# Attention, then a GRU, on one core: v of fourteen batches by seven quarter products, x normalised in place, and one root moved

## The chip, the cores and the metric

The kernel runs on one core of one Trainium2 chip. The metric is the device time of one execution in microseconds (us). TensorE (PE) multiplies, VectorE (DVE), ScalarE (ACT) and GpSimd (POOL) do the element work, and SyncE (SP) issues the transfers. Everything is float32.

## The reference

The input `x` has 16 batches of 256 tokens with 512 features; `cond` has one row of 512 for each batch. An adaptive normalisation and an attention with 16 heads of 32 come first, then a GRU over the 256 tokens:

```python
scale, shift = split(cond @ W_emb + b_emb)
xn = rms_norm(x, g_norm) * (1 + scale) + shift
q, k, v = split_heads(xn @ W_qkv)              # 512 -> 3 * 512
attn = softmax(rms_norm(q, g_q) @ rms_norm(k, g_k).T * 32 ** -0.5)
o = merge_heads(attn @ v)
x = x + o + o @ W_out

def cell(h, x):                                # scanned over the tokens
    r, z, n = gates(x @ W_ih + b_ih, h @ W_hh + b_hh)
    return (1 - z) * n + z * h
x = x + scan(cell, cond, x)
```

## The kernel before

The program has two parts. The attention part takes the first third of the time and goes batch by batch; the GRU part takes the rest, one token after the other. The order on PE, DVE, ACT and POOL is written out by hand: each engine does its instructions in the order in which the source issues them, and waits where data or a buffer is not ready. Transfers go through SP's queue in their order of issue.

In the attention part, the loop over `b` runs four slots for each batch, one for each group of four heads. A slot begins with the logits of its group (`logits_by_key`, L703), whose exponentials ScalarE takes (`exps_by_key`, L717), while GpSimd adds the two halves of each exponential (`sums`, L719). The group of the slot before (`prev`) is weighed with v (`weigh_by_key`, L731, L741), and VectorE divides by the sum: two transposes and a reciprocal (`put_weighed_by_key`, L755 to L759), and the product into `oT` (`finish_weighed_by_key`, L765). That last step frees the PSUM bank X of the weighing.

Beside this, each slot prepares part of the next batch `m = b + 1` and the turning of batch `b + 2`. From batch 2 on, q and k are not projected directly. The product of 256 tokens by 512 features with the weights is cut into halves in each direction, and seven products of quarters (`multiply`, L346) take the place of eight, after the scheme of Strassen and Winograd. The sums that this takes stand in `w_sums` (of the weights, made once: `make_w_sum`) and `x_sums` (of x, four for each batch, S1 to S4: `make_x_sum`, L336), all by GpSimd. `keep` (L358) copies partial results from PSUM, `add_kept` (L363) adds them. The next batch's first product `z` goes to PSUM bank A, `q7` to bank Y, `q2` to bank X. v is projected directly (`project`, L269): 32 matmuls of 128x512 a batch.

The quarters of q and k are normalised by head. ScalarE squares them (`square`, L390), VectorE sums the squares (`sum_heads`, L394). The root (`Rsqrt`) has a first half (L190 on VectorE, L192 and L193 on ScalarE) and a second half of three small VectorE operations (L197, L198, L200, named `u` and `y`). `norm_quarters` then multiplies (L373), transposes into `qkT` (L379), and lets GpSimd scale (L386).

x itself: `load_x` loads a batch, `norm_first` (L216) squares and sums it on ScalarE, `norm_apply` (L227) writes the normalised x to a buffer `xs` in `w_a`, `turn_x` (L242) transposes it on TensorE, and `put_x` (L259, L261) scales and shifts it into `xnT`. In `w_a` the halves of `squares` are the output of the squares of q and k; the squares of x, of which only the sum is used, go to `xs`.

The gains decide at run time whether the exponentials are bounded; with the inputs used they are, and of the two programs in the file the one with `bounded` true runs.

Of the kernel before, what the change touches and what calls it, by code (L numbers as in the profile page):

```python
# [20 lines left out]
def kernel(  # L21
# [99 lines left out]
    def program(ctx, bounded):  # L121
# [4 lines left out]
        small = work.enter_context(tc.tile_pool(name="small", bufs=4))  # L126
# [12 lines left out]
        xs = w_a[:, KC * 2 * D : KC * 2 * D + NT * D].rearrange("p (n d) -> p n d", n=NT)  # L139
        squares = w_a[:, KC * 2 * D + NT * D : KC * 3 * D].rearrange("p (i n) -> p i n", i=2)  # L140
        wih = w_a.rearrange("p (k n) -> p k n", k=KC)
        w_sums = w_a[:, 0 : 3 * 2 * D].rearrange("p (i k c) -> p i k c", i=3, k=2)
        x_sums = w_a[:, 3 * 2 * D : 4 * 2 * D].rearrange("p (i k t) -> p i k t", i=4, k=2)

# [64 lines left out]
        def norm_first(b, parts=range(NT)):  # L209
            if parts[0] == 0:  # L210
                batches[b].ssx = small.tile([P, NT], F32, tag="ssx", name=f"ssx_{b}")
                batches[b].rs = Rsqrt(batches[b].ssx, D, NT, f"x{b}")
            for n in parts:

                unused = xs[:, n, :] if b != 2 else spare(f"squares_{n}")
                nc.scalar.activation(  # L216
                    unused, x_tiles[b][n], AF.Square,
                    accum_out=batches[b].ssx[:, n : n + 1],
                )
# [5 lines left out]
        def norm_apply(b, rstd):  # L225
            for n in range(NT):
                nc.vector.tensor_scalar(  # L227
                    xs[:, n, :], x_tiles[b][n], rstd[:, n : n + 1],
                    None, ALU.mult,
                )  # L230
            if 0 < b and b + 2 < B:
                load_x(b + 2)
# [11 lines left out]
        def turn_x(b, banks):  # L244
            batches[b].xnT = p1.tile([P, KC, T], F32, tag="xnT", name=f"xnT_{b}", bufs=2)
            tps = [tile_ps(f"tpx_{b}_{r}", banks[r], (P, KC, NT, QR)) for r in range(R)]
            for c in range(KC):
                for n in range(NT):
                    turn_block(
                        [tp[:, c, n, :] for tp in tps], xs[:, n, c * P : (c + 1) * P]  # L250
                    )
            return tps
# [55 lines left out]

        T2, T3, T4, T1 = range(4)
# [6 lines left out]
        def make_w_sum(i):  # L316
            if i == T3:
                add_weights(w_sum(T3), w_half(1, 1), ALU.subtract, w_half(0, 1))
            elif i == T2:
                add_weights(w_sum(T2), w_sum(T3), ALU.add, w_half(0, 0))  # L320
            elif i == T4:
                add_weights(w_sum(T4), w_half(1, 0), ALU.subtract, w_sum(T2))
            else:
                add_weights(w_half(0, 1), w_half(0, 1), ALU.subtract, w_half(0, 0))
# [13 lines left out]
        def multiply(a, stationary, w, name=None):  # L338
            start = isinstance(a, str)
            if start:  # L340
                a = tile_ps(name, a)
            w = w.rearrange("p k s (g j d) -> p k j s g d", j=HG, d=DH)
            for k in range(2):
                for i in range(4):
                    for j in range(HG):
                        nc.tensor.matmul(  # L346
                            a[32 * j : 32 * j + 32, i * P : (i + 1) * P],
                            stationary[:, k, 32 * i : 32 * i + 32],
                            w[:, k, j],
                            start=(start and k == 0 and i == 0),  # L350
                            stop=(k == 1),
                            skip_group_check=True,
                        )
            return a

# [32 lines left out]
        def square(b, n, s, a):  # L388
            sq = spare(f"sq_{b}_{n}_{s}") if b == 0 else squares[:, s]
            nc.scalar.activation(sq, a, AF.Square)  # L390
            return sq
# [357 lines left out]
        def put_weighed_by_key(w, finish=True):  # L749


            if w is None:
                return
            den = p1.tile([P, T // DH, DH], F32, tag="den", name=f"den_{w.b}_{w.g}")
            nc.vector.transpose(den.rearrange("p a b -> p (a b)"), w.o[:, 1, :])  # L755
            inv = small.tile([P, T // DH, 1], F32, tag="inv", name=f"inv_{w.b}_{w.g}")
            nc.vector.reciprocal(inv, den[:, :, 0:1])
            rden = p1.tile([P, T], F32, tag="rden", name=f"rden_{w.b}_{w.g}")
            nc.vector.transpose(rden, inv.to_broadcast([P, T // DH, DH]))  # L759
            w.rden = rden  # L760
            if finish:
                finish_weighed_by_key(w)
# [23 lines left out]
        def first_slot1(b, w, prev, st):  # L786
            m = b + 1
            exps_by_key(w)
            make_w_sum(T2)
            project_qk(m, 0, 1, (3,), st.k)  # L790
# [11 lines left out]
        def first_slot2(b, w, prev, st):  # L802
# [8 lines left out]
            for i in (S3, S1, S2, S4):  # L811
                make_x_sum(m + 1, i)
            put_weighed_by_key(prev)
# [32 lines left out]

        def quarter_slot0(b, w, prev, st):
# [3 lines left out]
            project(b, 1, 2, (2, 3), st.v1)  # L851
            put_v(b, 1, st.v1)
            tpx = turn_x(b + 2, ("lg2", "lg3")) if b + 2 < B else None
            put_weighed_by_key(prev)
            if tpx:
# [11 lines left out]
        def quarter_slot1(b, w, prev, st):  # L867
            m = b + 1
            exps_by_key(w)
            multiply(st.z, x_sums[:, S1], w_half(0, 1))  # L870
            weigh_by_key(prev, "X")
            z4 = keep(m, 4, st.z)
            st.c22 = add_kept(m, 1, 1, st.q7, z4)
            put_weighed_by_key(prev)
            multiply(st.z, x_sums[:, S4], w_half(1, 1))
            sq = st.sa.square(1, st.c22)
            st.v0 = project(m, 0, 2, (0,), "Z")
            if m + 1 < B:
                make_x_sum(m + 1, S3)
            st.sa.add(1, sq)  # L880
# [7 lines left out]
        def quarter_slot2(b, w, prev, st):  # L888
# [11 lines left out]
            project(m, 0, 2, (1, 2, 3), st.v0)  # L900
            if m + 1 < B:
                make_x_sum(m + 1, S1)
                make_x_sum(m + 1, S2)
            st.sb.add(1, sq)
            finish_weighed_by_key(prev)
            if b + 3 < B:
                batches[b + 3].rs.first()
            put_v(m, 0, st.v0)
            st.sb.rs.first()
            st.rb = st.sb.rs.second()  # L910
            if b == 2:
# [4 lines left out]
        def quarter_slot3(b, w, prev, st):  # L916
# [3 lines left out]
            weigh_by_key(prev, "X")  # L920
            st.v1 = project(m, 1, 2, (0, 1), "Z")
# [3 lines left out]
            if m == B - 1:  # L925
# [3 lines left out]
                load_rows(wih, w_ih)  # L929
                project(m, 1, 2, (2, 3), st.v1)  # L930
                put_v(m, 1, st.v1)
            else:
                make_x_sum(m + 1, S4)
                begin_quarters(m + 1, st)
# [143 lines left out]
        def fast_last_batch(prev):  # L1078
            w = logits_by_key(B - 1, 0)
            for g in range(NG):  # L1080
                exps_by_key(w, sums=False)
                weigh_by_key(prev, "YZ"[g % 2], sums=(g == 0))
# [18 lines left out]
        with tc.manual_schedule(engines=ORDERED):  # L1101
# [29 lines left out]
            load_x(2)  # L1131
            tpx = turn_x(0, ("lg0", "lg1"))
            emb = small.tile([P, 8, 32], F32, tag="emb", name="emb", bufs=1)
# [36 lines left out]
            norm_first(2)  # L1170
            if bounded:
                batches[2].rs.first()
            turn_qk(0, 1, norm_qk(0, 1, accs[1], s1.rs.second()))
# [27 lines left out]
            (fast_last_batch if bounded else last_batch)(prev)  # L1201
# [226 lines left out]
```

## Time and profile before

| | before |
|---|---|
| median of 3 runs | 1636.08 us (1634.75 to 1636.09) |
| the profiled execution | 1636.28 us, span 1634.4 us |
| granted TensorE clock | 0.998 |
| logits of the first batch begin | 36.12 us |
| period of a batch, from b = 1 on | 29.91 us (one of 29.99) |
| first product of the GRU part (L944) | 500.9 us |
| busy in the 29.90 us from 251.05 | PE 29.90, DVE 21.32, ACT 17.43, POOL 16.90 us |

A row of the profile's lists names an engine, a line of the program, the operation, output<-inputs and their sizes. A float32 matmul leaves two rows. The lengths of TensorE's rows overlap, so the time that a group costs is read from its start to the start of the next group.

### The profile page before, as it was taken

The page shows a single profiled execution, that of the slowest core. Times are in us where ns is not written, and L with a number is a line of the kernel's source. Part 1 is how long each engine was busy: PE and PEld are TensorE (multiplying, and loading weights), DVE is VectorE, ACT ScalarE, POOL GpSimd, SP SyncE. Part 2 cuts the span into 40 slices and gives each one's busy share as a digit, 9 for nine tenths or more (in the row PEclk, how much of TensorE's full clock was granted, in tenths as well). Part 3 has the DMA queues.
Part 4 walks back from the last instruction along what each step waited for, and adds up shares of the span by engine and source line. Part 5 has one row for each costly group of instructions (what it writes and reads, how often), then busy time and mean ns, then how long its engine had stood idle before and what let it go on. Part 6 is the DMA issues. An engine that isn't in the chain of part 4 may idle for free.

```text
span 1634.4 us, 99580 instructions
## 1 busy us (share of the span) xinstructions
PE 1616.0 (99%) x45590; PEld 1308.3 (80%) x45590; DVE 954.2 (58%) x3102; ACT 560.8 (34%) x1770; POOL 342.5 (21%) x626
## 2 busy tenths in 40 slices
PE   8999999999999999999999999999999999999997
PEld 4566766767767888888888888888888888888886
DVE  4677677676665555555555555555555555555554
ACT  3565665565643222222222222222222222222222
POOL 0655556465550000000000000000000000000000
PEclk9999999999999999999999999999999999999999
DMA  5100001000042000000000000000000000000000
GB/s 217 29 17 22 24 16 29 16 16 27 18 116 70 11 23 21 20 17 17 18 23 23 18 17 17 20 21 23 17 18 17 21 20 17 10 11 11 17 11 18
DMA packets 51409, 44.71 MB, mean 27 GB/s; under 512 B 10615, under 2 KB 43683, under 8 KB 50979
## 3 DMA queue, kind: packets, MB, share of 16 engines
q1 hardware_dynamic: 50889, 38.20, 8.6%
q8 instruction: 358, 5.87, 1.5%
q14 instruction: 72, 0.59, 0.1%
q10 hardware_dynamic: 90, 0.06, 0.0%
HBM read 29.79 MB, written 8.39 MB: 23 GB/s over the span
## 4 chain that ended last, share of the span: by engine, by line
PE 68%; DVE 1%; issue 0%; ACT 0%; DVEq 0%; POOL 0%; ACTq 0%
PE gr L983 27%; PE gz L983 20%; PE gn L983 14%; PE o L1217 6%; PE first L944 0%; PE lg L703 0%; PE o L731 0%; DVE trh L1266 0%; PE o L741 0%; ACT n L1345 0%; DVE n L1344 0%; DVE n L1343 0%; DVE padded L1372 0%; DVE padded L1371 0%; DVE padded L1373 0%
## 5 line engine op out<-in xcount | busy, mean ns | idle before, releaser
L983 PE MATMUL gr<-w_a,xT 128*32 128x256 f32 x4096 | 267.7, 379 | 0.0
L1339 ACT ACTIVATE r<-trr 128x64 f32<-128x64 f32 x256 | 65.4, 256 | 514.4 <-DVE trr L1266 512.6
L1266 DVE STREAM_TRANSPOSE trr<-gr 128x128 f32<-128x128 f32 x256 | 81.0, 317 | 274.7 <-PE gr L983 274.6
L719 POOL TENSOR_TENSOR sums<-e 128x256 f32<-128x256 f32 x240 | 183.0, 793 | 221.8 <-ACT e L717 221.8
L983 PEld LDWEIGHTS gr<-w_a,xT 128*32 128x32 f32 x4096 | 132.8, 110 | 85.1
L1345 ACT ACTIVATE n<-n 128x64 f32<-128x64 f32 x256 | 65.6, 256 | 309.2 <-DVE n L1344 306.3
L1375 POOL TENSOR_TENSOR y<-xT,padded 128x64 f32<-128x64 f32 x128 | 41.1, 321 | 531.5 <-DVE padded L1373 531.5
L1266 DVE STREAM_TRANSPOSE trh<-gn 128x128 f32<-128x128 f32 x256 | 81.0, 317 | 117.3 <-PE gn L983 117.3
L717 ACT ACTIVATE e<-lg 128x512 f32<-128x512 f32 x256 | 131.9, 603 | 45.5 <-PE lg L703 45.3
L1217 PE MATMUL o<-oT,wo 128*32 128x256 f32 x1920 | 147.2, 379 | 0.0
L1375 POOL TENSOR_TENSOR y<-xT,h 128x64 f32<-128x64 f32 x127 | 40.7, 320 | 501.0 <-DVE h L1373 501.0
L983 PE MATMUL gr<-w_b,padded 128*32 128x128 f32 x4096 | 135.7, 273 | 2.4 <-DVE padded L1373 1.4
L983 PEld LDWEIGHTS gr<-w_b,padded 128*32 128x32 f32 x4096 | 114.6, 110 | 29.1 <-DVE padded L1373 28.6
L983 PE MATMUL gz<-w_b,padded 128*32 128x128 f32 x4096 | 135.3, 273 | 0.0
L983 PE MATMUL gn<-w_b,padded 128*32 128x128 f32 x4096 | 135.3, 273 | 0.0
L983 PE MATMUL gz<-w_a,xT 128*32 128x128 f32 x4096 | 135.3, 273 | 0.0
L983 PE MATMUL gr<-w_b,h 128*16 128x128 f32 x4064 | 134.3, 273 | 0.5 <-DVE h L1373 0.2
L983 PEld LDWEIGHTS gz<-w_a,xT 128*32 128x32 f32 x4096 | 117.1, 110 | 21.8
L983 PE MATMUL gz<-w_b,h 128*16 128x128 f32 x4064 | 134.2, 273 | 0.0
L983 PE MATMUL gn<-w_b,h 128*16 128x128 f32 x4064 | 134.2, 273 | 0.0
L269 PE MATMUL qkv<-w_b,xnT 128*32 128x512 f32 x1024 | 122.1, 596 | 0.1
L983 PEld LDWEIGHTS gn<-w_b,padded 128*32 128x32 f32 x4096 | 114.5, 110 | 0.0
(154 smaller groups left out, 2540.2 us busy)
## 6 DMA issues: line engine op xcount, KB each, us to landing
xin<-in_x_dram SPq DMA_DIRECT2D x256, 32.0 KB, 2.7
out_dram<-osb SPq DMA_DIRECT2D x248, 32.0 KB, 2.5
x<-in_x_dram SPq DMA_DIRECT2D x28, 256.0 KB, 2.9
w_b<-in_L_cond_W_qkv_dram SPq DMA_DIRECT2D x4, 768.0 KB, 8.5
w_a<-in_L_cond_W_ih_dram SPq DMA_DIRECT2D x16, 192.0 KB, 6.6
w_a<-in_L_cond_W_emb_dram SPq DMA_DIRECT2D x4, 512.0 KB, 5.3
w_b<-in_L_cond_W_hh_dram SPq DMA_DIRECT2D x16, 128.0 KB, 4.1
oT<-in_x_dram SPq DMA_DIRECT2D x2, 512.0 KB, 8.6
```

Source lines behind the costliest of these rows:

```text
L269: nc.tensor.matmul(a[32 * j : 32 * j + 32, :], batches[b].xnT[:, k, n * P + 32 * j : n * P + 32 * j + 32], wq[:, k, s * D : (s + 1) * D], ...
L717: nc.scalar.activation(w.e[i], w.lg[i], AF.Exp)
L719: nc.gpsimd.tensor_tensor(w.sums[:, i, :], w.e[i][:, 0, :], w.e[i][:, 1, :], ALU.add)
L983: nc.tensor.matmul(dst[32 * j : 32 * j + rows], stationary, w[:, k, :].rearrange("p (g j c) -> p j g c", g=3, c=P)[:, j, first::2][:, : ds ...
L1217: nc.tensor.matmul(acc[32 * j : 32 * j + 32, :], w[:, k, P * j + 32 * m : P * j + 32 * m + 32], rhs, start=(k == 0), stop=(k == KC - 1),)
L1266: nc.vector.transpose(tr.rearrange("p q s b -> p (q s b)"), gate)
L1339: nc.scalar.activation(r, turned("r", t, gr[:, 0, :])[:, :, s, :], AF.Sigmoid)
L1345: nc.scalar.activation(n, n, AF.Tanh)
L1375: (nc.gpsimd if t + 1 < T else nc.vector).tensor_tensor(y[:, :, tl * B : (tl + 1) * B], xTs[grp][:, :, ti, :], h, ALU.add)
```

## The change

v of the batches 2 to 15 is formed by seven quarter products too. `multiply_v` does one: eight matmuls of 128x256. `w_sums_v` holds three sums of v's weights, made once on GpSimd in the first two batches. The seven products are spread over the slots: two each in slots 1, 2 and 3, the last (`end_v`) in slot 0 of the batch itself. `keep_v` copies three partial results from PSUM on ScalarE, GpSimd adds the first of them to two others, and VectorE forms three quarters of v (`add_v` and slot 3). The next batch's `z` in slot 3 stands between the fifth and the sixth v product. In slot 1 the last step of the weighing is issued after the sum of squares instead of before.

The room for `w_sums_v` comes from `xs`: x is normalised in place, and the squares of x go into the buffers of the squares of q and k, one in `w_a` and one in a pool. Batch `b + 2`'s buffer is loaded anew after `turn_x` instead of after `norm_apply`. In the first part, the first half of the third x's root stands behind the norm of the second half of the tokens. `emb` and `rden` share the buffer of `den`.

```diff
-        xs = w_a[:, KC * 2 * D : KC * 2 * D + NT * D].rearrange("p (n d) -> p n d", n=NT)
-        squares = w_a[:, KC * 2 * D + NT * D : KC * 3 * D].rearrange("p (i n) -> p i n", i=2)
+        squares = [w_a[:, KC * 3 * D - D : KC * 3 * D]]
+        if bounded:
+            squares.append(p1.tile([P, D], F32, name="squares"))
...
+        w_sums_v = w_a[:, 4 * 2 * D : 11 * D].rearrange("p (i k c) -> p i k c", i=3, k=2)
@@ norm_first
-                unused = xs[:, n, :] if b != 2 else spare(f"squares_{n}")
                 nc.scalar.activation(
-                    unused, x_tiles[b][n], AF.Square,
+                    squares[n], x_tiles[b][n], AF.Square,
                     accum_out=batches[b].ssx[:, n : n + 1],
                 )
@@ norm_apply
-                    xs[:, n, :], x_tiles[b][n], rstd[:, n : n + 1],
+                    x_tiles[b][n], x_tiles[b][n], rstd[:, n : n + 1],
                     None, ALU.mult,
                 )
-            if 0 < b and b + 2 < B:
-                load_x(b + 2)
@@ turn_x
+            if 1 < b and b + 2 < B:
+                load_x(b + 2)
             return tps
@@
+        def multiply_v(a, stationary, w, start=False):
+            for k in range(2):
+                for j in range(4):
+                    nc.tensor.matmul(
+                        a[32 * j : 32 * j + 32, :],
+                        stationary[:, k, 32 * j : 32 * j + 32],
+                        w[:, k],
+                        start=(start and k == 0),
+                        stop=(k == 1),
+                        skip_group_check=True,
+                    )
+
+        def keep_v(b, i, a):
+            z = p1.tile([P, T], F32, tag=f"kept_v{i}", name=f"kept_v_{b}_{i}")
+            nc.scalar.copy(z, a)
+            return z
...
+        def end_v(b, st):
+            multiply_v(st.v7, x_part(b, 1, 1), v_sum(T4))
+
+        def add_v(b, st):
+            nc.vector.tensor_tensor(v_quarter(b, 0, 1), st.vz, st.vz1, ALU.add)
+            nc.vector.tensor_tensor(v_quarter(b, 1, 0), st.v7, st.vz2, ALU.add)
@@ quarter_slot0
-            project(b, 1, 2, (2, 3), st.v1)
-            put_v(b, 1, st.v1)
+            if b == 1:
+                project(b, 1, 2, (2, 3), st.v1)
+                put_v(b, 1, st.v1)
+            else:
+                end_v(b, st)
             tpx = turn_x(b + 2, ("lg2", "lg3")) if b + 2 < B else None
             put_weighed_by_key(prev)
+            if b > 1:
+                add_v(b, st)
+                make_x_sum(m, S4)
@@ quarter_slot1
             multiply(st.z, x_sums[:, S1], w_half(0, 1))
+            first_v = tile_ps(f"v1_{m}", "Z")[:, 0:T]
+            multiply_v(first_v, x_part(m, 0, 0), v_half(0, 0), start=True)
             weigh_by_key(prev, "X")
             z4 = keep(m, 4, st.z)
+            st.vz1 = keep_v(m, 1, first_v)
+            multiply_v(first_v, x_part(m, 0, 1), v_half(1, 0))
             st.c22 = add_kept(m, 1, 1, st.q7, z4)
-            put_weighed_by_key(prev)
+            put_weighed_by_key(prev, finish=False)
             multiply(st.z, x_sums[:, S4], w_half(1, 1))
-            sq = st.sa.square(1, st.c22)
-            st.v0 = project(m, 0, 2, (0,), "Z")
-            if m + 1 < B:
-                make_x_sum(m + 1, S3)
-            st.sa.add(1, sq)
+            st.sa.add(1, st.sa.square(1, st.c22))
+            finish_weighed_by_key(prev)
+            nc.scalar.copy(v_quarter(m, 0, 0), first_v)
@@ quarter_slot2
-            project(m, 0, 2, (1, 2, 3), st.v0)
+            vs = tile_ps(f"v_{m}", "Z")
+            st.vz, st.v7 = vs[:, 0:T], vs[:, T : 2 * T]
+            multiply_v(st.vz, x_sums[:, S2], v_sum(T2), start=True)
+            multiply_v(st.v7, x_sums[:, S3], v_sum(T3))
             if m + 1 < B:
-                make_x_sum(m + 1, S1)
-                make_x_sum(m + 1, S2)
+                make_x_sum(m + 1, S3)
             st.sb.add(1, sq)
             finish_weighed_by_key(prev)
+            st.vz2 = keep_v(m, 2, st.vz)
+            nc.gpsimd.tensor_tensor(st.vz2, st.vz2, st.vz1, ALU.add)
             if b + 3 < B:
                 batches[b + 3].rs.first()
-            put_v(m, 0, st.v0)
@@ quarter_slot3
-            weigh_by_key(prev, "X")
-            st.v1 = project(m, 1, 2, (0, 1), "Z")
+            if m == B - 1:
+                multiply_v(st.vz, x_sums[:, S1], v_half(0, 1))
+                weigh_by_key(prev, "X")
+            else:
+                weigh_by_key(prev, "X")
+                multiply_v(st.vz, x_sums[:, S1], v_half(0, 1))
+                make_x_sum(m + 1, S1)
+                make_x_sum(m + 1, S2)
+                st.z = multiply("A", x_part(m + 1, 0, 0), w_half(0, 0), f"z_{m + 1}")
+            z4 = keep_v(m, 4, st.vz)
+            nc.gpsimd.tensor_tensor(z4, z4, st.vz1, ALU.add)
+            multiply_v(st.vz, x_sums[:, S4], v_half(1, 1))
             put_weighed_by_key(prev)
             if b + 3 < B:
                 norm_apply(b + 3, batches[b + 3].rs.second())
+            nc.vector.tensor_tensor(v_quarter(m, 1, 1), st.v7, z4, ALU.add)
-            if m == B - 1:
+            if m < B - 1:
+                st.q7 = multiply("Y", x_sums[:, S3], w_sum(T3), f"q7_{m + 1}")
+                st.z1 = keep(m + 1, 1, st.z)
+            else:
...
-                load_rows(wih, w_ih)
-                project(m, 1, 2, (2, 3), st.v1)
-                put_v(m, 1, st.v1)
-            else:
-                make_x_sum(m + 1, S4)
-                begin_quarters(m + 1, st)
+                load_rows(wih, w_ih, (0, 1))
@@ fast_last_batch
+                if g == 0:
+                    end_v(B - 1, st)
+                    add_v(B - 1, st)
+                    load_rows(wih, w_ih, (2, 3))
@@ the first part
             load_x(2)
+            load_x(3)
...
             norm_first(2)
+            turn_qk(0, 1, norm_qk(0, 1, accs[1], s1.rs.second()))
             if bounded:
                 batches[2].rs.first()
-            turn_qk(0, 1, norm_qk(0, 1, accs[1], s1.rs.second()))
```

`make_v_sum(T3)`, `(T2)` stand in the slots 1 and 2 of batch 0, `(T1)`, `(T4)` in the slots 1 and 2 of batch 1; `v_half` and `v_sum` name a half of v's weights and a sum.

## The prediction

> **What bounds the kernel now.** I read the page first, then TensorE's timeline for one batch of the steady part, then all engines in the same window, and last the places where VectorE (DVE) and GpSimd (POOL) meet.
>
> ```profile
> span 1634.4 us, 99580 instructions
> PE 1616.0 (99%) x45590; PEld 1308.3 (80%) x45590; DVE 954.2 (58%) x3102; ACT 560.8 (34%) x1770; POOL 342.5 (21%) x626
> ```
>
> TensorE is busy 99% of the span, so saved matmul time counts, unless something makes TensorE wait instead. The change touches the attention part alone (to about 501 us). There the batches repeat exactly every 29.91 us, in four slots that each begin with the logits (`lg`). One batch on TensorE (columns: start, length, engine, line, operation, output<-inputs, shapes, count):
>
> ```profile
> 221.14 1.15 PE L703 MATMUL lg<-qkT 32*128 32x256 f32 x16
> 222.22 1.07 PE L731 MATMUL o<-e,v 128*32 128x256 f32 x16
> 223.11 0.61 PE L741 MATMUL o<-sums,ones 128*32 128x256 f32 x8
> 223.54 1.90 PE L269 MATMUL qkv<-w_b,xnT 128*32 128x512 f32 x16
> 225.37 0.71 PE L242 MATMUL tpx<-ident,w_a 64*128 64x64 f32 x16
> 226.01 1.95 PE L346 MATMUL q<-w_b,xnT 128*32 128x128 f32 x64
> ...
> 235.53 1.04 PE L269 MATMUL qkv<-w_b,xnT 128*32 128x512 f32 x8
> 236.50 1.15 PE L703 MATMUL lg<-qkT 32*128 32x256 f32 x16
> ...
> 240.64 2.76 PE L269 MATMUL qkv<-w_b,xnT 128*32 128x512 f32 x24
> 243.33 1.15 PE L703 MATMUL lg<-qkT 32*128 32x256 f32 x16
> 244.41 1.07 PE L731 MATMUL o<-e,v 128*32 128x256 f32 x16
> ```
>
> No row carries an idle mark: TensorE never waits here. Lengths overlap, so I cost by start to start. The slots begin at 221.14, 229.64, 236.50, 243.33 and 251.05: 8.50, 6.86, 6.83 and 7.72 us. VectorE and GpSimd in the same window show how little room that leaves:
>
> ```profile
> 224.99 0.60 DVE L765 TENSOR_TENSOR oT<-o,rden 128x256 f32<-128x256 f32 x1
> ...
> 243.62 0.58 DVE L765 TENSOR_TENSOR oT<-o,rden 128x256 f32<-128x256 f32 x1
> 243.71 0.73 POOL L336 TENSOR_TENSOR w_a<-w_a,xnT 128x256 f32<-128x256 f32 x1
> ...
> 244.06 0.41 DVE L190 TENSOR_SCALAR m_x<-ssx 128x2 f32<-128x2 f32 x1
> ...
> 245.24 0.69 DVE L373 TENSOR_TENSOR c<-z,y_qk 128x512 f32<-128x512 f32 x1
> ```
>
> L765 frees bank X at 225.59 for the `q` product of 226.01 (0.4 us to spare), and at 244.20 for the weighing of 244.41 (0.2 us). L373 frees bank A at 245.93 for the `z` product of 247.44 (1.5 us). TensorE is the bound, VectorE is next by tenths.
>
> The third reading is from batch 0, where POOL happens to work beside VectorE's small root operations:
>
> ```profile
> 63.93 2.81 POOL L719 TENSOR_TENSOR sums<-e 128x256 f32<-128x256 f32 x4 [1.38 <-ACT e L717]
> 63.95 0.76 DVE L198 TENSOR_TENSOR u_qk<-u_qk,m_qk 128x32 f32<-128x32 f32 x1
> 64.74 0.66 DVE L200 SCALAR_TENSOR_TENSOR y_qk<-u_qk,y_qk 128x32 f32<-128x32 f32 x1
> ```
>
> Both take 0.19 us elsewhere. Each waits until one GpSimd add of the four ends: 0.57 and 0.47 us lost, one after the other. L190, L197 and L373 with both operands in SBUF show the same (0.41 for 0.17, 0.63 for 0.16, 1.16 for 0.68); operations that read PSUM do not.
>
> **TensorE work.** Out go 32 matmuls 512 wide a batch: start to start 1.83 (slot 0), 0.97 (slot 1), 2.69 (slot 2) and 1.72 (slot 3), 7.21 us. In come 7 products of 8 matmuls 256 wide, 16 rows each. The nearest rows are L288 (same stationary and weights; 16 rows in 0.88 us at 48.41) and L731 (0.86 to 0.89): 0.86 to 0.89 us each, I take 0.865, 6.05 us. A matmul ahead of `lg` or `tpx` takes 0.11 us more (L346 1.86 instead of 1.75); three of the old groups had that and three places of the new order have it, so 6.38 us. Saving 0.83 us a batch (0.66 to 0.86). By slots, without waits: slot 0 7.64 (one product), slot 1 7.73 (two), slot 2 5.98 (two), slot 3 7.73 (two); sum 29.08. Over 14 batches 11.6 us: the gain on offer.
>
> **Wait A, slot 0.** The `q` product needs bank X, which L765 frees 225.59 - 221.14 = 4.45 us into the slot. TensorE gets there at 4.87 now, at 2.40 + 0.97 + 0.64 = 4.01 after: it waits 0.45 to 0.6. I take 0.5; slot 0 is 8.15.
>
> **Wait B, slot 3.** The change moves the last step of the weighing in slot 1 behind the sum of squares, so VectorE's order changes there, but its root for the first pair of quarters comes at the same time (16.5 us into the batch), and from there to L765 of slot 2 (end 23.07 us into the batch) it works without a pause. TensorE now needs bank X at 23.26, after at 8.15 + 7.73 + 5.98 + 1.08 = 22.94. Wait 0.2 (0.1 to 0.35).
>
> **Wait C, slot 3, the largest.** The next batch's first product `z` now stands before the sixth v product, and needs bank A, which L373 `c<-z` still reads. Ahead of that on VectorE stand L190 twice, L197, L198 and L200, all with operands in SBUF. Today GpSimd is idle from 244.45 to 245.23, so they take 1.15 us. After, GpSimd has no such hole, for two reasons. (1) The squares of x now go into the buffers of the q/k squares. ScalarE's square of x in slot 1 must wait for VectorE's L394 to have read that buffer: it starts at about 17.3 us into the batch instead of 16.28, with four exponentials queued behind it, and the four sums of GpSimd wait for those: they run from about 18.6 to 21.9, not 17.55 to 20.89. (2) Behind them come two scalings (0.92), S3 (0.73) and the new add into `kept_v` (0.73), to 24.2, and there slot 3's sums begin, to 27. So VectorE's chain from 23.0 meets S3 (0.35 lost), the new add (0.5), and two sums (0.5, 0.47): 1.8 us. Bank A, free at 24.79 today (of which the first L190's wait of 0.24 is part already), is free at 26.35 to 26.5. TensorE arrives at 22.94 + 0.2 + 0.89 + 0.43 + 0.86 = 25.3: wait 1.1. With only two collisions it is nothing to 0.3, with a whole add (0.6) lost at all five 2.3.
>
> The SBUF page of the Trainium skill (SBUF — State Buffer, "Who interferes with whom") says that whichever of the two issues first holds the shared port pair for its whole instruction and the other fully blocks, for `tensor_tensor` with two SBUF inputs too. By that rule each of five steps could lose an add's full 0.73 us, and the sum would be 3.6 us instead of the rows' 1.8; the rows of batch 0 show less, since the start of an operation runs beside the other engine. It speaks against adding GpSimd work just here.
>
> **Sum of a steady batch.** 8.15 + 7.73 + 5.98 + (7.73 + 0.2 + 1.1) = 30.9 against 29.91: +1.0, and up to 1.1 with the upper values of A. Thirteen periods (b = 1 to 13) give 13 to 14.5 us; I take 14, since A's arrival is reckoned without the 0.03 to 0.1 us that a release takes to reach TensorE.
>
> **What lies beside other work.** ScalarE: two copies of 0.59 out, four 256 wide in (about 0.37 by L1253's 128x256), +0.3 on 17.4 busy of 29.9; nothing, unless exponentials become late (logits would wait one for one). VectorE: three adds of 128x256 from PSUM, 0.42 each by L1249 (0.60 by L765): two behind L765 in slot 0, ahead of `put_x`, whose results are used only in the next batch, one before slot 0's reciprocal, where VectorE idles 2.2 us. GpSimd: eight weight adds once (0.73 each), two adds a batch, counted in C. Loads of x: they are issued behind the transposes instead of behind the norm, some 5 us later on SP's queue, with a whole batch until the first reader and 2.9 us to land: nothing (if that cover were gone, 2.9 us once). The last batch's weights for the second part: two halves, the later one still some 15 us before its use, with 6.6 us to land; if late, up to 3 us.
>
> **Start.** Moving the third x's root behind the norm lets `qkT` be ready earlier: up to 2.1 of the 2.38 us that `lg` waits at 36.12. Against that, batch 0's root chain now meets the first v sums on GpSimd (three losses of 0.5 to 0.6) and the weighing of slot 1 waits 1.0 to 1.3. Batches 1 and 2, with weight adds still on GpSimd, add 0.3 and up to 1.3. Together 0.5 (-1.5 to +2.5).
>
> **Total.** 14 + 0.5 = 14.5 us. The profiled execution took 1636.28 us (span 1634.4 and 1.9 around it), the median is 1636.08; I add to the median: 1650.6 us, +0.9%. No change means within 0.2%, 3.3 us, about what a measurement of this kernel can tell.
>
> **Rivals.**
> - The chain slips past GpSimd, C vanishes, A and B stay: 0.83 - 0.7, a gain of 0.1 a batch; with the start, 1632 to 1638. For it: in the steady batches `u` and `y` keep 0.19 us today, and a shift of 0.1 us decides which engine goes first. Against: two losses in a row in batch 0, and no hole left on GpSimd. 7%.
> - Faster: TensorE's saving arrives whole, since all three frees move forward as the slots shorten: 1636.1 - 11.6, with the start about 1624 (1622 to 1632). It decides if L765 ends 0.5 us earlier in slots 0 and 2. Against: VectorE starts on the weighing's end and has no pause to give. 8%.
> - All five small steps lose a full add: wait C 2.3 or more, +2.1 to +2.3 a batch: 1663 to 1668. For it: GpSimd's queue is full from 18.6 to 27. Against: 0.47 to 0.57 is what the rows show of one loss. 5%.
> - The forecast, 1640 to 1662: 80%.
>
> The range runs from 1640 to 1662; 5% lies above it, 15% below. Slower by over 0.2%: 0.80 + 0.05 = 0.85. Within 0.2%: 0.06 of the first rival's 0.07. Faster: 0.08 and the rest of the first rival, 0.09.
>
> **What will show it.** On TensorE: groups of 16 rows 128x256 in 0.86 to 0.89 for the v products; period about 30.9, slots 8.15, 7.73, 5.98, 9.0; idle marks before `q` and before the weighing in slot 3, released by DVE `oT`, and before `z`, released by DVE `c`, the last the largest. On VectorE: u and y steps of 0.6 to 0.7 in slot 3. I am wrong if TensorE has no idle marks, if `u` and `y` keep 0.19 us, or if the v products take over 0.95 us.

## The result and the profile after

The changed kernel takes 1658.17 us (median of 4 runs, 1657.03 to 1659.6) against 1636.09 us of the kernel before in the same measurement: ratio 1.0137, 95% interval 1.012 to 1.0155. It is 22 us slower. The forecast was 1650.6 us with a range of 1640 to 1662; the value is inside, 7.6 us above the forecast. The profiled execution took 1659.6 us, span 1657.8 us, which is 23.4 us more than the span before.

In the changed kernel the line numbers are shifted: logits L735 (before L703), weighing L763 and L773, `multiply` L358, `multiply_v` L371, the step that frees bank X L797, the normalisation of q and k L405, the square of x L219, the first half of the root L194, its second half L201, L202, L204, the sums of exponentials L751, the sums of x L348, the new GpSimd adds L961 and L987, `keep_v`'s copy L382.

The head of the page, then the list of waits on TensorE (engine, tile and line that waited <- what it waited for: us in total, how often, the longest):

```profile
span 1657.8 us, 101083 instructions
PE 1609.4 (97%) x46262; PEld 1334.0 (80%) x46262; DVE 994.9 (60%) x3144; ACT 567.1 (34%) x1798; POOL 363.9 (22%) x662
```

```profile
PE z L358 <- DVE c L405: 18.8, 12, 2.3
PE q L358 <- DVE oT L797: 7.2, 13, 1.1
PE o L763 <- PE lg L735: 2.4, 10, 0.2
PE lg L735 <- POOL qkT L418: 1.4, 1, 1.4
```

TensorE's busy time fell by 6.6 us (1616.0 to 1609.4) while the span grew. The saving arrived and was more than eaten by three waits in nearly every batch: those that the prediction called C, A and B, in this order of size. The third row names TensorE itself as releaser, but its logits had ended by then (283.97 us in the batch below); the weighing needs bank X, which L797 on VectorE freed later, at 284.07, 0.14 us before the weighing began.

Rows of one steady batch of the changed kernel from the timeline (start, length, engine, line, operation, tiles, shapes, count, and in brackets the idle time before it with its releaser):

```profile
260.89 1.15 PE L735 MATMUL lg<-qkT 32*128 32x256 f32 x16
...
264.74 0.59 DVE L797 TENSOR_TENSOR oT<-o,den 128x256 f32<-128x256 f32 x1
...
265.48 1.96 PE L358 MATMUL q<-w_b,xnT 128*32 128x128 f32 x64 [0.51 <-DVE oT L797]
...
269.11 1.15 PE L735 MATMUL lg<-qkT 32*128 32x256 f32 x16
...
271.96 1.05 PE L371 MATMUL v<-w_b,xnT 128*32 128x256 f32 x16
...
272.82 1.05 PE L763 MATMUL o<-e,v 128*32 128x256 f32 x16
...
276.84 1.15 PE L735 MATMUL lg<-qkT 32*128 32x256 f32 x16
...
278.33 0.63 ACT L219 ACTIVATE w_a<-x 128x512 f32<-128x512 f32 x1 [0.75 <-DVE ssqk L426]
...
279.61 3.28 POOL L751 TENSOR_TENSOR sums<-e 128x256 f32<-128x256 f32 x4 [5.81 <-ACT e L749]
...
282.82 1.15 PE L735 MATMUL lg<-qkT 32*128 32x256 f32 x16
...
283.49 0.58 DVE L797 TENSOR_TENSOR oT<-o,den 128x256 f32<-128x256 f32 x1
...
283.75 0.74 POOL L348 TENSOR_TENSOR w_a<-xnT 128x256 f32<-128x256 f32 x1
283.92 0.60 DVE L194 TENSOR_SCALAR m_x<-ssx 128x2 f32<-128x2 f32 x1
...
284.21 1.07 PE L763 MATMUL o<-e,v 128*32 128x256 f32 x16 [0.24 <-PE lg L735]
284.43 0.79 DVE L194 TENSOR_SCALAR m_qk<-ssqk 128x32 f32<-128x32 f32 x1
284.44 0.74 POOL L961 TENSOR_TENSOR kept_v<-kept_v,kept_v 128x256 f32<-128x256 f32 x1
...
285.13 2.80 POOL L751 TENSOR_TENSOR sums<-e 128x256 f32<-128x256 f32 x4
285.14 0.79 DVE L201 SCALAR_TENSOR_TENSOR u_qk<-y_qk 128x32 f32<-128x32 f32 x1
...
285.96 0.65 DVE L202 TENSOR_TENSOR u_qk<-u_qk,m_qk 128x32 f32<-128x32 f32 x1
286.65 0.65 DVE L204 SCALAR_TENSOR_TENSOR y_qk<-u_qk,y_qk 128x32 f32<-128x32 f32 x1
...
287.33 0.69 DVE L405 TENSOR_TENSOR c<-z,y_qk 128x512 f32<-128x512 f32 x1
...
288.08 1.96 PE L358 MATMUL z<-w_b,xnT 128*32 128x128 f32 x64 [1.50 <-DVE c L405]
```

Start to start, the slots take 8.22, 7.73, 5.98 and 9.75 us (the next batch's logits begin at 292.57), 31.68 us in all. The rows at 271.96 and 272.82 show one v product: 0.86 us to the next group. From 283.75 to 287.30 VectorE and GpSimd go turn by turn: each of the five small steps ends 0.02 to 0.05 us after one of GpSimd's adds, and the next step begins within 0.1 us of that end. All of them together set the end of `c<-z`, for which TensorE stands 1.5 us by its mark, 1.7 us start to start.

Where the 23.4 us of span lie, from the starts of the logits:

| stretch | before | after | difference |
|---|---|---|---|
| up to the first logits | 36.12 | 34.10 | -2.0 |
| batch 0 | 35.41 | 35.12 | -0.3 |
| batches 1 and 2 | 59.90 | 64.49 | +4.6 |
| batches 3 to 13 | 329.0 | 348.4 | +19.4 |
| batch 14 | 28.10 | 28.19 | +0.1 |
| last batch, to the first product of the GRU part | 12.41 | 14.09 | +1.7 |
| the GRU part | 1133.5 | 1133.4 | -0.1 |

The last 1.7 us are of another kind. Windows around the last batch's first logits of the changed kernel (length in us; busy us with counts of TensorE, its weight loads, VectorE, ScalarE and GpSimd; the granted TensorE clock; the DMA's share and GB/s):

```profile
506.00:510.34 4.34, 2.59 (x47) 1.07 (x37) 4.13 (x9) 1.78 (x5) 4.21 (x7) 1.00 0.98 213
510.34:514.40 4.06, 4.06 (x44) 2.10 (x48) 1.09 (x3) 2.07 (x4) 0.64 (x1) 0.58 0.33 81
514.40:518.00 3.60, 3.60 (x68) 2.00 (x60) 2.36 (x6) 1.44 (x3) 0.00 (x0) 1.00 0.61 158
```

TensorE idles for the last 1.44 us of the first window, waiting for `qkT`, and in the second its granted clock is 0.58 on average: half speed for about 3.4 us (0.42 times 4.06, divided by 0.5). The logits take 1.70 us there instead of 1.15, the weighing 1.94 instead of 1.07.

### The profile page after: what moved, and what is told of

It is laid out like the page before. It is cut to its first block, busy times and chain, and to the rows that moved or that the text cites. A ratio compares the mean times of both kernels' runs of the same rounds, so it can differ in the third digit from the quotient of the medians.

```text
span 1657.8 us, 101083 instructions
## 1 busy us (share of the span) xinstructions
PE 1609.4 (97%) x46262; PEld 1334.0 (80%) x46262; DVE 994.9 (60%) x3144; ACT 567.1 (34%) x1798; POOL 363.9 (22%) x662
## 4 chain that ended last, share of the span: by engine, by line
PE 67%; DVE 1%; issue 0%; ACT 0%; DVEq 0%; ACTq 0%
PE gr L1049 26%; PE gz L1049 19%; PE gn L1049 14%; PE o L1291 6%; PE first L1010 0%; PE o L763 0%; PE lg L735 0%; DVE trh L1340 0%; ACT n L1419 0%; PE o L773 0%; DVE n L1417 0%; DVE n L1418 0%; DVE padded L1445 0%; DVE padded L1446 0%; DVE padded L1447 0%
## 5 line engine op out<-in xcount | busy, mean ns | idle before, releaser
L751 POOL TENSOR_TENSOR sums<-e 128x256 f32<-128x256 f32 x240 | 175.6, 763 | 205.4 <-ACT e L749 205.4
L1049 PEld LDWEIGHTS gz<-w_b,padded 128*32 128x32 f32 x4096 | 114.5, 110 | 0.0
```

The source lines that it names most:

```text
L751: nc.gpsimd.tensor_tensor(w.sums[:, i, :], w.e[i][:, 0, :], w.e[i][:, 1, :], ALU.add)
L1049: nc.tensor.matmul(dst[32 * j : 32 * j + rows], stationary, w[:, k, :].rearrange("p (g j c) -> p j g c", g=3, c=P)[:, j, first::2][:, : ds ...
```

## The experiments

Six of the runs (no adds, add late, squares late, `z` late, slot 0 exchanged, x's root behind) have one execution each, the profiled one, so their periods are what is compared.

**Is wait C the new GpSimd add?** Leave out GpSimd's two adds into `kept_v` (parts of v then lack a term):

```diff
-            nc.gpsimd.tensor_tensor(st.vz2, st.vz2, st.vz1, ALU.add)
...
-            nc.gpsimd.tensor_tensor(z4, z4, st.vz1, ALU.add)
```

> The changed kernel without GpSimd's two adds of vz1 (into vz2 and into z4), so that parts of v are wrong. Port theory: wait C is the sum of what VectorE's chain m_x, m_qk, u, u, y loses to GpSimd's operations in slot 3 (0.43 + 0.62 + 0.60 + 0.46 + 0.46 = 2.57 us in the profile after). Without the add between S3 and the sums GpSimd has its hole of 0.7 us again, the chain loses m_x's 0.4 alone, u and y are back at 0.19, slot 3 falls from 9.75 to about 8.1, the period from 31.68 to 30.0 to 30.2, the time by 20 to 23 us to about 1637. Order theory (z stands one product too early in the list of TensorE, whatever GpSimd does): the wait before z stays above 1.2 us, the period at 31.2 or more.

Period 30.02 us, slot 3 8.10 us, 1642.23 us. One line of its waits is enough; the twelve waits have become two:

```profile
PE z L358 <- DVE c L405: 2.8, 2, 1.5
```

So these adds, 0.73 us each on GpSimd, cost TensorE 1.65 us in each batch. The total stays above the expected 1637 us, since batches 1 and 2 (31.98 and 31.47 us) keep most of their loss and the GRU part took 1.9 us longer in this execution.

**Does its place do it, or its amount?** The same add, issued behind the exponentials of the next slot:

```diff
@@ quarter_slot2
-            nc.gpsimd.tensor_tensor(st.vz2, st.vz2, st.vz1, ALU.add)
@@ quarter_slot3
             exps_by_key(w)
+            nc.gpsimd.tensor_tensor(st.vz2, st.vz2, st.vz1, ALU.add)
```

> The changed kernel with GpSimd's add into vz2 issued behind the four sums of slot 3 instead of ahead of them; all work is kept. Port theory: what counts is where the add stands, not that it is made, so this is worth as much as leaving both adds out: slot 3 about 8.1 to 8.2, period 30.0 to 30.2, time 1637 to 1640. Load theory (GpSimd simply has too much work in a batch): no more than 0.1 us a batch, period 31.6.

Period 30.02 us, slot 3 8.10 us, 1642.71 us: as without the adds. It is the place. The total is above the expected 1637 to 1640 us, because here, too, batches 1 and 2 keep most of their loss, and because the late add makes the last batch's `qkT` wait: TensorE stands 2.13 us there, its clock is half for 6.8 us behind that, and the last stretch takes 15.5 us.

**Do the squares of x drive GpSimd into the chain?** The prediction held that ScalarE's square of x, waiting for a buffer in slot 1 (0.75 us in the row at 278.33), makes the exponentials and GpSimd's sums late. Here both squares go to slot 2, the add stays where the change put it:

```diff
@@ quarter_slot1
-            if b + 3 < B:
-                norm_first(b + 3, (0,))
@@ quarter_slot2
             if b + 3 < B:
-                norm_first(b + 3, (1,))
+                norm_first(b + 3)
```

> The changed kernel with both squares of x on ScalarE in slot 2 behind the exponentials, so that no square waits for VectorE's reading of the shared buffer ahead of the exponentials. Port theory: the exponentials of slot 2 start about 1 us earlier, so do GpSimd's sums, scalings, S3 and the add; they end about 23.3 us into the batch, and VectorE's chain meets m_x's neighbour alone: slot 3 about 8.1 to 8.3, period 30.0 to 30.3, time 1637 to 1641. If the shared buffer is of no matter: period 31.6 to 31.7.

Period 30.10 us, slot 3 8.17 us, 1641.05 us. VectorE's chain and GpSimd in slot 3 of a steady batch of this kernel, from the timeline:

```profile
334.91 0.73 POOL L348 TENSOR_TENSOR w_a<-xnT 128x256 f32<-128x256 f32 x1
335.59 0.73 POOL L959 TENSOR_TENSOR kept_v<-kept_v,kept_v 128x256 f32<-128x256 f32 x1
335.94 0.40 DVE L194 TENSOR_SCALAR m_x<-ssx 128x2 f32<-128x2 f32 x1
336.26 0.17 DVE L194 TENSOR_SCALAR m_qk<-ssqk 128x32 f32<-128x32 f32 x1
336.34 0.18 DVE L201 SCALAR_TENSOR_TENSOR u_qk<-y_qk 128x32 f32<-128x32 f32 x1
336.56 0.19 DVE L202 TENSOR_TENSOR u_qk<-u_qk,m_qk 128x32 f32<-128x32 f32 x1
336.78 0.19 DVE L204 SCALAR_TENSOR_TENSOR y_qk<-u_qk,y_qk 128x32 f32<-128x32 f32 x1
336.83 3.27 POOL L751 TENSOR_TENSOR sums<-e 128x256 f32<-128x256 f32 x4 [0.51 <-ACT e L749]
```

The add is still there, but GpSimd comes to it earlier, is done at 336.32, and then waits 0.51 us for the exponentials. In that hole four of the five steps run at 0.17 to 0.19 us; only `m_x` loses time. The wait needs both parts of the change: the add, which fills the hole, and the late sums, which push the add to where the hole was.

**Which step counts how much?** The root of x's third following batch moves behind the norm of the quarters, one small step fewer in the chain:

```diff
@@ quarter_slot2
-            if b + 3 < B:
-                batches[b + 3].rs.first()
@@ quarter_slot3
             norm_quarters(m, ((0, 1), (1, 0)), (st.z, st.c21), st.rb, (True, False))
+            if b + 3 < B:
+                batches[b + 3].rs.first()
```

> The changed kernel with the first half of x's root (m_x) behind norm_quarters in slot 3, so one step fewer in VectorE's chain ahead of c<-z. Port theory: each step of the chain costs one turn of the port, and a step fewer is worth a turn, 0.4 to 0.7 us, of which 0.17 is its own work: slot 3 9.05 to 9.35, period 30.9 to 31.3, time 1648 to 1653. If the chain's length counted only by its own work: 0.17 us, slot 3 at 9.6, period 31.5.

Period 30.98 to 31.0 us, slot 3 9.05 to 9.09 us, 1649.3 us. A step of 0.17 us that is taken out gives TensorE 0.66 to 0.70 us: its turn of the alternation goes with it. In the changed kernel the five steps last 0.60, 0.79, 0.79, 0.65 and 0.65 us against 0.17, 0.17, 0.19, 0.19 and 0.19: 0.43 + 0.62 + 0.60 + 0.46 + 0.46 = 2.57 us lost.

**The z product later.** `z` goes behind the sixth v product:

```diff
@@ quarter_slot3
-                st.z = multiply("A", x_part(m + 1, 0, 0), w_half(0, 0), f"z_{m + 1}")
...
             multiply_v(st.vz, x_sums[:, S4], v_half(1, 1))
+            if m < B - 1:
+                st.z = multiply("A", x_part(m + 1, 0, 0), w_half(0, 0), f"z_{m + 1}")
```

> The changed kernel with z behind the sixth v product again. Port theory: VectorE's chain is as long as before (u and y 0.6 to 0.8 us), TensorE comes to z 0.87 us later, so the wait falls from 1.7 to about 0.85: slot 3 8.9 to 9.0, period 30.8 to 31.0, time 1646 to 1650. Order theory: the wait is gone, slot 3 at 8.0, period 29.9 to 30.1, time 1635 to 1638.

Period 30.83 us, slot 3 8.90 us, 1650.22 us. Slot and period are the expected ones, the reason is not. The wait before `z` is gone but for 0.1 us, and the sixth v product waits in its place, for ScalarE's copy of the fifth out of the same bank:

```profile
PE v L371 <- ACT kept_v L382: 6.9, 14, 0.5
```

The two limits nearly coincide: in a steady batch `c<-z` ends at 284.86 us and `z` starts at 284.92, so VectorE's chain would have held it there without the copy as well. This run therefore cannot tell the two apart by its time. It shows what `z` stood there for: it covers that copy.

**Wait A alone.** The product that waits for bank X in slot 0 changes places with a product that needs no bank X:

```diff
@@ slot 0
+            if b > 1:
+                multiply(st.z, x_sums[:, S2], w_sum(T2))
+                st.z2 = keep(m, 2, st.z)
             a = multiply("X", x_part(m, 0, 1), w_half(1, 0), f"q2_{m}")
...
-            multiply(st.z, x_sums[:, S2], w_sum(T2))
-            st.z2 = keep(m, 2, st.z)
+            if b == 1:
+                multiply(st.z, x_sums[:, S2], w_sum(T2))
+                st.z2 = keep(m, 2, st.z)
```

> The changed kernel with the product q2 (bank X) behind z's second product in slot 0, from batch 2 on. Wait A is a wait for bank X alone, 0.5 us, and z's second product (bank A, 1.77 us) covers it: slot 0 falls from 8.22 to 7.6 to 7.65, the other slots stay at 7.73, 5.98 and 9.75, period 31.0 to 31.1, time 7 to 8 us less, 1650 to 1651. Rival: q2's result, its square and its sum come 1.8 us later and the exponentials of slot 1 behind them, and slot 1 or slot 3 takes the 0.6 us back: period 31.5 to 31.7.

Slot 0 7.64 us, the other slots unchanged (7.73, 5.98, 9.75), period 31.10 us, 1648.29 us. Wait A was 0.58 us, and 7.64 is what the prediction gave the slot without waits. The total is below the expected 1650 us because the last batch kept its clock in this execution (12.46 us for its last stretch instead of 14.09).

**The start.** The kernel before, with nothing but the third x's root moved:

```diff
-            if bounded:
-                batches[2].rs.first()
             turn_qk(0, 1, norm_qk(0, 1, accs[1], s1.rs.second()))
+            if bounded:
+                batches[2].rs.first()
```

> The kernel before with one part of the change alone: the first half of the third x's root behind the norm in the first part. The logits of batch 0 begin 2.0 us earlier (34.1 instead of 36.12 us) as in the profile after, and all from there on is as before; if the shorter wait also keeps the clock of batch 0 (0.95 before, 1.00 after), 0.5 us more. Time 2.0 to 2.6 us less, 1633.5 to 1634.1, ratio 0.9985. Rival: batch 0's own chains take it back, no change (within 0.5 us).

1633.06 us (median of 11 runs) against 1636.0 us, ratio 0.9985 (0.9976 to 0.9994): 2.9 us faster, more than the 2.0 us by which the first logits come earlier. Batch 0 takes 33.76 us instead of 35.41. The windows of the kernel before, and below them those of this run, show why:

```profile
33.00:36.12 3.12, 0.74 (x9) 0.01 (x1) 2.95 (x8) 0.72 (x1) 0.00 (x0) 1.00 0.10 26
36.12:40.00 3.88, 3.88 (x32) 1.75 (x36) 1.88 (x6) 0.03 (x1) 0.00 (x0) 0.56 0.08 18
```

```profile
31.00:34.10 3.10, 2.92 (x32) 0.75 (x28) 2.93 (x9) 2.85 (x8) 0.00 (x0) 1.00 0.07 15
34.10:38.00 3.90, 3.90 (x60) 2.18 (x64) 1.96 (x6) 1.69 (x4) 0.52 (x1) 1.00 0.13 31
```

Before, the 2.38 us of idle TensorE ahead of the first logits were followed by the same 3.4 us at half clock; with 0.2 us of the wait left, the clock stays whole, and batch 0 gains 1.65 us.

**All three repairs, all work kept:** squares in slot 2, the slot 0 products exchanged, the add behind the exponentials.

> The changed kernel with three moves and all work kept: the add into vz2 behind the sums of slot 3, both squares of x in slot 2 behind the exponentials, q2 behind z's second product. Port theory and wait A add up: slots 7.6, 7.73, 5.98, 8.15, period 29.45 against 29.91 before; thirteen periods give 0.46 each, 6 us, less 2 to 4 us in batches 1 and 2 (weight adds on GpSimd), 2 us gained at the start, up to 1.7 us lost if the clock falls at the last batch again: 1630 to 1634, ratio 0.9965 to 0.999. If the three moves hit the same wait and no more is to be had than e3: 1637 to 1641.

1632.58 us (median of 11 runs) against 1636.0, ratio 0.9982 (0.9973 to 0.9991). Slots 7.64, 7.73, 5.98 and 8.16, period 29.51 us: 0.40 of the 0.83 us saved, 0.43 still lost ahead of the weighing of slot 3. It is only 0.5 us below the kernel before with the root moved, within the spread of either: the 0.40 us a batch are spent on batch 0 (35.13 for 33.76), on batches 1 and 2 (31.21 and 30.24) and on the half clock of the last batch, which is here too.

**Is it the idle engine that halves the clock?** The changed kernel, with products of the identity in the last batch's wait:

```diff
         def fast_last_batch(prev, st):
+            warm_up("A", 6)
             w = logits_by_key(B - 1, 0)
```

> The changed kernel with one thing added: six TensorE products of the 128x128 identity, into a bank that nobody reads then, just ahead of the last batch's first logits. Twenty-four such products took 5.0 us at the start of the changed kernel (0.21 us each), so six take 1.25 us and fit into the 1.44 us for which TensorE waits there for GpSimd's qkT. Theory (the idle engine is what halves the granted clock for 3.4 us, and that is 1.7 us of the loss): the first logits still start 0 to 0.2 us after GpSimd's qkT, the clock stays at 1.00 behind them, the logits, weighing and sums take 1.15, 1.07 and 0.61 us in place of 1.70, 1.94 and 0.87, the stretch from the last batch's first logits to the first projection takes 12.3 to 12.5 us in place of 14.1, and the median falls from 1658.2 to 1656.3 to 1656.8. Rival (the clock falls there for another reason, at a set time or from the load before): the clock still halves, the stretch stays at 14.1 and the median at 1657.9 to 1658.5.

```profile
509.13 1.60 PE L1087 MATMUL warm_A<-ident 128*128 128x128 f32 x12
510.67 1.15 PE L735 MATMUL lg<-qkT 32*128 32x256 f32 x16
511.75 1.07 PE L763 MATMUL o<-e,v 128*32 128x256 f32 x16
512.63 0.61 PE L773 MATMUL o<-sums,ones 128*32 128x256 f32 x8
```

In the trace it does what was expected: clock 1.00, the three groups at 1.15, 1.07 and 0.61 us, the last stretch 12.46 us, the span 1656.4 instead of 1657.8. The median does not fall: 1658.04 us (4 runs, 1657.71 to 1660.18), as the rival has it.

The traces show where the clock falls. The length of a wait does not decide it: the waits of `z` in batch 2 of the changed kernel (2.30 us, to 129.22 us) and of three other runs (2.13 to 2.34 us) were followed by full clock, and so were its waits of 1.5 us in the other batches; the wait of 1.4 to 1.5 us ahead of the last batch was followed by half clock in two traces (the changed kernel, squares late) and not in four. But where a trace has two stretches at half clock, they begin a whole number of 3.413 us apart (in the kernel before at 36.26 and 1630.28 us, 467 times; in the four others 335 or 336 times). Two windows of this grid in the changed kernel, each with the window behind it:

```profile
507.38:510.80 3.42, 1.67 (x28) 0.87 (x28) 3.28 (x7) 0.40 (x2) 3.42 (x6) 1.00 0.92 205
510.80:514.21 3.41, 3.41 (x40) 1.56 (x36) 0.67 (x2) 2.07 (x4) 0.17 (x1) 0.50 0.29 69
125.09:128.50 3.41, 1.83 (x36) 0.99 (x27) 3.34 (x7) 1.80 (x4) 3.12 (x5) 1.00 0.00 0
128.50:131.91 3.41, 2.69 (x84) 2.35 (x88) 3.27 (x8) 0.58 (x1) 1.41 (x3) 1.00 0.02 5
```

By the profile, which models the ends of matmuls, TensorE was busy for 0.488 of the first window and for 0.535 of the third. Every trace ends in half clock, and its grid can be counted back from there. In all thirteen traces the clock fell after every window in which TensorE was busy for 0.488 or less, and after none with 0.490 or more; no run moved this bound on its own. What lets the clock rise again is not shown: with the late add it stayed half through a second window in which TensorE was busy for 0.85. The grid lies differently in each execution, so whether a wait costs the clock is chance. As an estimate, a window of 3.41 us slid over TensorE's busy times lies under 0.489 at the wait of the kernel before in 0.68 of all positions, at the last batch of the changed kernel in 0.18, at its batch 2 in 0.65. The filler takes away the rarer place and leaves batch 2, so this median could hardly show it. By this estimate the half clock of the last batch costs the changed kernel 0.3 us on average; that was not measured.

The mean clocks agree where they can be read. Half of 3.4 us in 1657 lowers the mean by 0.001, but each profile also ends in 4.6 to 7.2 us of half clock, so the mean alone does not tell. Of the 21 executions of the kernel before that stand beside the repaired kernel, nine have 0.999 and take 1634.47 to 1634.97 us, twelve have 0.997 or 0.998 and take 1635.86 to 1637.22 us: 12 of 21, where the estimate has 0.68. In this run the two do not go together: the profiled execution has 0.999 and 1658.31 us, two others 0.998 and 1657.71 and 1657.77 us.

**The same filler where the wait is longer,** nine products in the repaired kernel's 2.1 us:

> The repaired kernel (square halves in the third slot, key product's second quarter at the head of the first slot, v's GpSimd add behind the root chain) with nine such identity products (1.9 us at 0.21 us each) in the 2.12 us for which TensorE waits for qkT ahead of the last batch's first logits. Period unchanged at 29.51 us and the start unchanged. If the idle engine is what halves the clock: no half clock behind 482.8 us, the last stretch 12.3 to 12.5 us in place of 14.09, median 1630.7 to 1631.2 (repaired: 1632.58). If not: 1632.4 to 1632.8.

1630.83 us (median of 7 runs, 1630.42 to 1632.0), ratio 0.9972 (0.996 to 0.9983) against the kernel before. No half clock, the last stretch 12.45 us instead of 14.09, period unchanged. Six of the seven executions have a mean clock of 0.999; of the eleven without the filler three have, at 1630.68 to 1631.16 us, and the two at 0.996 are the longest, 1634.74 and 1634.77 us. The estimate fits: without the filler a window under 0.489 lies at this wait in 0.69 of all positions, with it in none. Here the idle engine is the cause.

**The best version:**

```diff
@@ quarter_slot2, beside the three repairs
-            if b == 1:
-                make_v_sum(T4)
-            elif b == 2:
+            if b == 2:
@@ quarter_slot3
             norm_quarters(m, ((0, 1), (1, 0)), (st.z, st.c21), st.rb, (True, False))
+            nc.gpsimd.tensor_tensor(st.vz2, st.vz2, st.vz1, ALU.add)
...
             nc.gpsimd.tensor_tensor(z4, z4, st.vz1, ALU.add)
+            if b == 1:
+                make_v_sum(T4)
@@ fast_last_batch
+            warm_up("A", 6)
```

> The repaired kernel with three edits more, all of the work kept: v's GpSimd add goes behind the whole of the scale steps of the fourth slot (so that it no longer stands ahead of GpSimd's qkT of the last batch, 0.7 us of TensorE's wait there), batch 1's fourth v sum of weights is made in its fourth slot behind z's add (it now stands in its second slot, ahead of sums that TensorE waits for; batch 1's period is 31.2 us against the others' 29.51), and six identity products stand in the wait that is left. Expected: period 29.5 us, batch 1 at 30.3 to 30.9 us, the wait ahead of the last batch's first logits 1.3 to 1.5 us, the last stretch 12.3 to 12.5 us if the idle engine halves the clock, and a median of 1629.0 to 1630.5 us, 0.35 to 0.45% under the kernel before. Rival (the clock falls anyway, and batch 1's time lies in waits that these sums do not set): 1631.5 to 1632.5.

1629.51 us (median of 5 runs, 1629.02 to 1631.1), ratio 0.9963 (0.9949 to 0.9976). Period 29.51 us, batch 1 30.37 us, last stretch 12.46 us. It beats both kernels: 6.5 us under the one before, 28.7 us under the changed one, and 3.5 us under the kernel before with the root moved. That last difference is what the rest of the change, v by seven products above all, brings once most of its waits are dealt with; the 0.43 us of slot 3 are still there.

## Why the prediction was right, and where it was off

- **TensorE's saving: right.** The v products take 0.86 us start to start, and slots 1 and 2, which have no wait, 7.73 and 5.98 us as worked out.
- **Wait A: right.** 0.58 us for 0.5 (slot 0 8.22 for 8.15), inside the 0.45 to 0.6.
- **Wait B: right,** 0.24 us by its mark for 0.2, and 0.31 start to start.
- **Wait C: the right mechanism, a term of the sum too small.** The term that was too small is "meets S3 (0.35 lost), the new add (0.5), and two sums (0.5, 0.47): 1.8 us". Five steps stand in the chain and four have a price; the sum does not say which one has none. All five lost, each to another GpSimd add, three sums among them: 2.57 us for 1.82. If the one without a price is the second L190, `m_qk`, that is 0.62 us of the difference, and the other four are off by 0.1 us at most. Wait C is 1.7 us for 1.1, so the period is 31.68 us for 30.9, and the thirteen periods cost 22.9 us for 14, not counting 1.1 us in batches 1 and 2 that the prediction put under the start. This is all of the miss and more.
- The Trainium skill (SBUF — State Buffer, "Who interferes with whom") says that the engine that comes second is blocked for the whole instruction of the first. By it the prediction reckoned 3.6 us for the five steps, by the rows 1.8 us. The trace shows 2.57 us, between the two: every step is held until an add ends, as the page says, but loses 0.43 to 0.62 us of a 0.73 us add, not all of it.
- **The two reasons for the missing hole: right.** The delayed squares (278.33 us, 17.4 us into the batch, predicted 17.3) and the new add are each necessary; taking either away brings the period to 30.0 to 30.1 us.
- **The start: two terms right in size, one missing.** The first logits come 2.0 us earlier (predicted up to 2.1). Batch 0 takes 1.36 us more than the kernel before with only the root moved (35.12 for 33.76; predicted 1.0 to 1.3), but not at the weighing of slot 1, as predicted: slots 0 and 1 keep their 9.57 and 6.83 us, slot 2 takes 0.60 us more and slot 3 0.76. Not foreseen was that the half clock behind the old wait goes too, 1.65 us. With 1.1 us more than a steady period in batches 1 and 2, the start is -1.2 us instead of +0.5.
- **The last batch: not foreseen.** The wait for `qkT` and the half clock behind it, 1.7 us in the profiled execution. That the start came out 1.7 us better than its term and the last batch 1.7 us worse, so that the two cancel, is luck.
- **The rivals.** The first (C vanishes) did not happen by itself, but two edits of a line or two make it happen. The second (faster) did not happen: waits A and B came in nearly every batch. The third, five collisions, is the nearest in kind: all five steps did lose, though less than a full add each.

## What to carry to other kernels

Where two engines hold each other up, as VectorE and GpSimd do here, count every small operation in the chain as one turn, the cheap ones too: a 0.17 us step that stands in a queue of 0.73 us adds costs 0.6 to 0.8 us. Before work is put on a lightly used engine (22% of the span here, but 16.9 of the 29.9 us of a batch already before the change), look whether the idle time that it fills is the hole in which another engine's critical chain runs; moving the new work by one group of instructions was worth 1.65 us a batch. And when a wait of TensorE goes, or comes, look at its granted clock behind it as well, and at how busy TensorE is around the wait rather than at the length of the wait alone.

## What was not expected of the hardware

- TensorE's granted clock was half for one or two stretches of 3.41 us after a wait in five of the thirteen traces. They begin on a grid of 3.413 us that lies differently in each execution, and the clock fell after the windows of this grid in which TensorE was busy for 0.488 or less; a wait of 2.3 us did without it where work stood close around it, and one of 1.44 us had it where other gaps were near. The price was 1.5 to 1.7 us for each stretch of 3.41 us. Executions of one kernel differ in it, and for the kernel before this makes most of their spread: about 1634.7 or about 1636.4 us. The Trainium skill (TensorE: Matmul & The Clock Gate, Part 1) describes windows of 3.4 us that run freely and decide the clock by how busy the engine was; the traces agree in the length and in the free run. The page has the clock fall after a whole idle window, and here less than that was enough.
- In slot 3 of the changed kernel VectorE and GpSimd, each with ready operations on SBUF, went strictly by turns, one instruction each (283.75 to 287.30 us). Even a `tensor_scalar` of 128x2 elements lost 0.43 us to an add of 128x256.
